# Moving the close of the state sums from VectorE to ScalarE and GpSimd, and six more convolutions to TensorE, in a fused attention, FFN, Mamba and LoRA block

## The chip, the core and the metric

The kernel runs on one core of a Trainium2 chip, in one launch. The metric is the device time of an execution in microseconds, the median over the runs. All arithmetic is fp32 (some matmuls split a value in two parts of fp32r).

## The reference

The input x is 4 x 256 x 512. A first layer adds a latent attention and an FFN of 1792 units; a second layer adds a Mamba block and a router with eight LoRA experts. The change touches only the Mamba block, which for each of the four sequences computes

```python
x, z = jnp.split(hidden_states @ in_proj_w, 2, axis=-1)      # 1024 channels each
for k in range(K):                                           # K = 4 taps in time
    xc = xc + conv_w[None, :, k:k + 1] * xp[:, :, k:k + Lq]
xc = silu(xc)                                                # xc began as conv_b
dt_r, Bm, Cm = rmsnorm of three parts of x_proj_w @ xc       # 32, 16, 16 rows
dt = softplus(dt_proj_w @ dt_r + dt_bias)
h = exp(dt * A) * h + dt * B_t * x_t                         # 16 states a channel, over 256 steps
y = sum over states of h * C_t
y = (y + D * xc) * silu(z)
out = y @ out_proj_w.T
```

## The kernel before

The order of all work is written out by hand: no scheduler moves an instruction, and each engine works its own queue in order. The first layer takes the first 330 us or so and is not touched. Its last matmuls (the FFN's second product, L469) run on into the first steps of what follows.

**Tiles of the Mamba block.** The 1024 channels of a sequence are eight chunks of 128 (DC = 8), and two chunks are a pair (p from 0 to 3). The 16 states are taken four at a time, so that a chunk is four steps (NU = 4) and a sequence 32 steps (PER). Step u belongs to sequence b = u // 32, chunk c = u % 32 // 4 and state group g = u % 4. There are 128 steps. In one step the 128 partitions hold 4 states x 32 channels, and the free axis 4 groups of channels x 256 points in time.

**One step** is, by engine:
- ScalarE: `decays`, four exponentials of 128 x 255 (L958), done two steps ahead, into one of three buffers;
- VectorE: `scan_in`, the product bx in PSUM (L964), then `scan`, the scan h over 128 x 1024 (L979); h has two buffers;
- GpSimd: hc = h * C (L984); hc has three buffers;
- TensorE: `states_sum`, one step later: four matmuls (L996), each of which sums the four states of 32 channels into its quarter of the one PSUM tile ysum. At a chunk's first step a matmul with the diagonal of D and xc (L994) opens ysum anew.

**The close.** When the four steps of a chunk are summed, `close_chunk` (L1000) multiplies ysum by silu(z) (tile sz, written by ScalarE in `gate_silu`, L932) on VectorE and writes the chunk of xcs over. It is issued between the product and the scan of the step two after the chunk's last one (u % 4 == 1). Until it is done TensorE can't open ysum for the next chunk. The output projection `out_mm` (L1088) reads the closed chunk.

**The next sequence's inputs.** While sequence b is scanned, the convolution of sequence b + 1 is made, in steps 5 to 20 of the 32:
- `px_mm` (L753): the input projection of a pair, into one PSUM tile px of 128 x 2 x 256;
- `conv_in`: ScalarE copies px to a padded tile (L762). For the pair's first chunk it scales the identity by the four taps, which gives four diagonals of 128 x 128 (L767). For the second chunk it writes the last tap with the bias (L768) and three scaled, shifted copies (L772);
- `conv_taps`, a step later: TensorE convolves the first chunk by four matmuls with the diagonals (L789), back into its half of px, and ScalarE adds the bias (L791). GpSimd adds the three copies of the second chunk (L795);
- `conv_silu` (L798), then the projection to dt, B and C: `pp_mm` (L809), `pp_square` (L815, L816), an inverse root on ScalarE (L708, L709) and on VectorE `pp_norm` (L823), which is issued after step 20's scan.

**Time steps.** `step_in` and `step_exp` (ScalarE) and `step_out` (GpSimd, L892 to L896, one instruction for each k) make dt for half a sequence; `step_x` (L903, GpSimd) makes du = dt * xc of a pair. Each sends its result to DRAM (L911), and `spread` (L917) loads it back in the layout of the steps, four DMAs for dt and four for du of a chunk, on SP's queue. On the same queue stand the loads of w_in (L621) and, in the first sequence, of the late weights rl, bw, lb and ow (L1206).

**The order** is two tables of step numbers, `at` (before the step's scan) and `late_at` (after it), filled by `put` and `put_late`; the main loop over u works them off.

Of the kernel before, what the change touches and what calls it, by code (L numbers as in the profile page):

```python
# [8 lines left out]
F32 = mybir.dt.float32  # L9

F32R = mybir.dt.float32r
AF = mybir.ActivationFunctionType
ALU = mybir.AluOpType
# [4 lines left out]
P = 128  # L18
B, S, D = 4, 256, 512
# [6 lines left out]
DIN, NST, KC, RK = 1024, 16, 4, 32  # L26
# [11 lines left out]
V_CW, V_CB, V_DB, V_AL, V_D, V_END = 0, 4, 5, 6, 22, 23  # L38
# [3 lines left out]
def block_kernel(  # L42
# [24 lines left out]
    nc = tc.nc  # L67
    mm = nc.tensor.matmul
# [15 lines left out]
    ident = cst[:, C_ID : C_ID + P]  # L84
# [34 lines left out]
    live = {}  # L119
# [22 lines left out]
    for i in range(2):  # L142
        t = ap1.tile([P, 2, 4, 32], F32, name=f"mpl{i}")
# [339 lines left out]
    def go(gen, n=1000):  # L483
        for _ in range(n):
            if next(gen, 1) == 1:
                break
# [138 lines left out]
    vec = we.tile([P, DC, V_END], F32, name="vec")  # L625
# [16 lines left out]
    w1 = ctx.enter_context(tc.tile_pool(name="w1", bufs=1, side="right"))  # L642
# [7 lines left out]
    NU = NST // NG  # L650
    PER = DC * NU
    xcs, nrms, dts, szs, crows = {}, {}, {}, {}, {}
# [27 lines left out]
    pads = []  # L680
    for i in range(2):
        t = w1.tile([P, 2, KC - 1 + S], F32, name=f"pad{i}")
# [12 lines left out]
    ysum = psy.tile([P, S], F32, name="ysum")  # L695
# [52 lines left out]
    def px_mm(b, p, i):  # L748
# [3 lines left out]
        for hc in range(HC):  # L752
            mm(px[:, i, :], lhsT=w[:, i, hc, :], rhs=xns[b][:, hc, :],  # L753
               start=(hc == 0), stop=(hc == HC - 1))

    def conv_in(b, p):


        px = live["px", b, p]
        if p == 0:  # L760
            xcs[b] = (act if b % 3 else w1).tile([P, DC, S], F32, tag=f"xc{b % 3}", name="xc")
        nc.scalar.copy(pads[p % 2][:, :, KC - 1 :], px)  # L762
        v = [vec[:, 2 * p + i, :] for i in range(2)]
        if b:
            dg = live["dg"] = w1.tile([P, KC, P], F32, tag="dg", name="dg")
            for k in range(KC):
                nc.scalar.activation(dg[:, k, :], ident, AF.Identity, scale=v[0][:, V_CW + k : V_CW + k + 1])  # L767
        nc.scalar.activation(xcs[b][:, 2 * p + 1, :], px[:, 1, :], AF.Identity,  # L768
                             bias=v[1][:, V_CB : V_CB + 1], scale=v[1][:, V_CW + KC - 1 : V_CW + KC])
        tp = w1.tile([P, KC - 1, S], F32, tag="tap", name="tap")  # L770
        for k in range(KC - 1):
            nc.scalar.activation(tp[:, k, :], pads[p % 2][:, 1, k : k + S], AF.Identity,  # L772
                                 scale=v[1][:, V_CW + k : V_CW + k + 1])
        live["tap"] = tp
        if b == 0:
            nc.scalar.activation(px[:, 0, :], px[:, 0, :], AF.Identity, bias=v[0][:, V_CB : V_CB + 1],
                                 scale=v[0][:, V_CW + KC - 1 : V_CW + KC])

    def conv_taps(b, p):
        px, c = live["px", b, p], 2 * p  # L780
        if b == 0:
            for k in range(KC - 1):
                nc.vector.scalar_tensor_tensor(
                    px[:, 0, :] if k < KC - 2 else xcs[b][:, c, :], pads[p % 2][:, 0, k : k + S],
                    vec[:, c, V_CW + k : V_CW + k + 1], px[:, 0, :], ALU.mult, ALU.add,
                )
        else:
            for k in range(KC):
                mm(px[:, 0, :], lhsT=live["dg"][:, k, :], rhs=pads[p % 2][:, 0, k : k + S],  # L789
                   start=(k == 0), stop=(k == KC - 1))  # L790
            nc.scalar.activation(xcs[b][:, c, :], px[:, 0, :], AF.Identity,  # L791
                                 bias=vec[:, c, V_CB : V_CB + 1])
        xc = xcs[b][:, c + 1, :]
        for k in range(KC - 1):
            nc.gpsimd.tensor_tensor(xc, xc, live["tap"][:, k, :], ALU.add)  # L795

    def conv_silu(b, z=None):
        nc.scalar.activation(xcs[b], xcs[b], AF.Silu)  # L798
# [143 lines left out]
    def lend(n, u):  # L942
        tag = lent[n][u]
        pool, bufs = (we, 3) if tag == "w_in" else (w1, 1)
        return pool.tile([P, NG, S], F32, tag=tag, name=n, bufs=bufs)

    def decays(u):
        b, c, g = u // PER, u % PER // NU, u % NU
        if u >= len(lent["d"]):
            da = decay[(u - 4) % 3]  # L950
        elif lent["d"][u] == "d":
            da = decay[0]
        else:
            da = lend("d", u)
            nc.gpsimd.memset(da[:, :, 0:1], 0.0)
        live["da", u] = da
        for k in range(NG):
            nc.scalar.activation(da[:, k, 1:], live["dts", b, c][:, k, 1:], AF.Exp,  # L958
                                 scale=aneg[:, c, k, g : g + 1])

    def scan_in(u):
        b, c, g = u // PER, u % PER // NU, u % NU
        bx = psx.tile([P, NG, S], F32, tag="bx", name="bx")
        nc.vector.tensor_tensor(  # L964
            bx, brow[g // 2][:, g % 2, :].unsqueeze(1).to_broadcast([P, NG, S]), live["dus", b, c], ALU.mult
        )
        live["bx"] = bx

    def scan(u, parts=1):
        b, c, g = u // PER, u % PER // NU, u % NU  # L970
        da, bx = live.pop(("da", u)), live["bx"]
        if u < len(lent["h"]):
            h, hc = lend("h", u), lend("hc", u)
        else:
            h = act.tile([P, NG, S], F32, tag="h", name="h", bufs=2)
            hc = act.tile([P, NG, S], F32, tag="hc", name="hc", bufs=3)
        for k in range(parts):
            n = slice(k * NG // parts, (k + 1) * NG // parts)
            nc.vector.tensor_tensor_scan(  # L979
                h[:, n].rearrange("p n t -> p (n t)"), da[:, n].rearrange("p n t -> p (n t)"),  # L980
                bx[:, n].rearrange("p n t -> p (n t)"), 0.0, ALU.mult, ALU.add,
            )

            (nc.vector if k == NG - 1 else nc.gpsimd).tensor_tensor(  # L984
                hc[:, n], h[:, n],
                crows[b][:, g, :].unsqueeze(1).to_broadcast([P, NG // parts, S]), ALU.mult,
            )
        live["hc", u] = hc
# [7 lines left out]
            mm(ysum[k * NB : (k + 1) * NB, :], lhsT=stack, rhs=hc[:, k, :],  # L996
               start=False, stop=(g == NU - 1))

    def close_chunk(b, c):
        nc.vector.tensor_tensor(  # L1000
            xcs[b][:, c, :], ysum, szs[b, c // 2][:, c % 2, :], ALU.mult
        )


# [82 lines left out]
    def out_mm(b, i, c):  # L1087
        mm(live["po", b, i], lhsT=xcs[b][:, c, i * P : (i + 1) * P], rhs=late_w["ow"][:, c, :],  # L1088
           start=False, stop=(c == DC - 1))
# [31 lines left out]
    px = live["px", 0, 3]  # L1121
    nc.scalar.copy(pads[1][:, :, KC - 1 :], px)
    for i in range(2):
        v = vec[:, 6 + i, :]
        nc.scalar.activation(px[:, i, :], px[:, i, :], AF.Identity, bias=v[:, V_CB : V_CB + 1],
                             scale=v[:, V_CW + KC - 1 : V_CW + KC])
# [33 lines left out]
    u, e, lw = live["u"], live["e"], live["lw"]  # L1160
# [15 lines left out]
    for i in range(2):  # L1176
        pdu = psmm.tile([P, 2, S], F32, tag="mm", name="pdus")
        for k in range(2):
            mm(pdu[:, k, :], lhsT=sel[:, (2 * i + k) * P : (2 * i + k + 1) * P], rhs=du[:, 0, :],
               start=True, stop=True)  # L1180
# [31 lines left out]
    def put(b, s, f, *a):  # L1212
        at.setdefault(b * PER + s, []).append((f, a))
# [5 lines left out]
    for b in range(B):  # L1219
# [36 lines left out]
        put(b, 2 if b else 6, step_in, b, 1, 1)  # L1256
        put(b, 3 if b else 7, step_exp, b, 1)

        for q, us in enumerate(((5, 6, 7), (10, 12, 14)) if b else ((8, 9, 11), (15, 17, 18))):
            for k in range(3):  # L1260
                put(b, us[k], step_out, b, 1, q, k)
        for p, u in ((2, 8 if b else 13), (3, 16 if b else 19)):
            put(b, u, step_x, b, p)
        for c in range(2, DC):
            o = 0 if b or c < 4 else 2
            put(b, 3 if c == 2 and not b else 4 * c - 6 + o, spread, "dt", b, c)
            put(b, 4 * c - 4 + o, spread, "du", b, c)
        put(b, 10, load_z, b, 2)
# [6 lines left out]
        if nxt < B:  # L1275
            o = 0 if b else 1
# [54 lines left out]
    total = B * PER  # L1331
    late = []
    for u in range(total + 2):
        if 3 <= u < total - 2:
            decays(u + 2)
        for f, a in at.get(u, ()):
            f(*a)
        if u < total:
            if u:
                scan_in(u)  # L1340
        last = u - 2
        if last >= 0 and last % NU == NU - 1:
            c = last % PER // NU
            close_chunk(last // PER, c)
            if last // PER == B - 1:
                late.append(c)
        if u < total:
            scan(u, 1 if u < total - 1 else 4)
            if u < 3:
                decays(u + 2)  # L1350
        for f, a in late_at.get(u, ()):
            f(*a)
        if late and u >= total - PER + 22:
            c = late.pop(0)
            for i in range(2):
                out_mm(B - 1, i, c)
        if 1 <= u <= total:
            states_sum(u - 1)
        if u < 3:
            go(ff, (9, 12, 100)[u])  # L1360
        if u == 2:
            open_act()
# [105 lines left out]
```

## Time and profile before

| | |
|---|---|
| runs | 850.30, 850.35 and 854.58 us; median 850.35 |
| profiled execution | 852.26 us, span 850.5 us, mean granted TensorE clock 0.954 |
| busy in the span | PE 740.6 (87%), VectorE (DVE) 669.6 (79%), ScalarE (ACT) 538.6 (63%), GpSimd (POOL) 489.1 (58%) |
| scan L979 | 125 of 128 x 1024, 2.284 us each |
| product L964 | 128, 1.232 us each |
| close L1000 | 32, 0.416 us each |
| hc L984 | 130, 2.322 us each |
| addition L795 | 45, 0.73 us each |

In a timeline a row has the start and the duration in us, the engine, the line, the operation, out<-in with their shapes, and how many instructions were merged; in brackets stands how long the engine was idle before it and what ended that. A row of waits has who waited for whom, the total in us, the times and the longest. A matmul of fp32 gives two records (x8 is four matmuls). The chain of waits is followed back from the last instruction.

### The profile page before, as it was taken

The numbers are of one execution on the slowest core, as the hardware profiler recorded it, in microseconds if no ns is written. First come the engines' busy times: TensorE is split into PE (matmuls) and PEld (weight loads), VectorE is DVE, ScalarE is ACT, GpSimd is POOL, SyncE is SP. The second block draws the span as 40 slices with busy tenths as digits, with TensorE's granted clock in tenths as the row PEclk, the third lists the DMA queues.
The fourth block names the chain that finished last, engine by engine and source line by source line (L and its number), as shares of the span: only waits on it lengthen the run. The fifth ranks groups of instructions, "written<-read, shape, count | busy, mean of one in ns | idle before, by whom it ended". The sixth has DMA issues, their size and how long they took to land.

```text
span 850.5 us, 10982 instructions
## 1 busy us (share of the span) xinstructions
PE 740.6 (87%) x3798; PEld 423.6 (50%) x3798; DVE 669.6 (79%) x647; ACT 538.6 (63%) x1061; POOL 489.1 (58%) x376
## 2 busy tenths in 40 slices
PE   5999999989999899989778888887898997956875
PEld 3565546656555676656444346344356444312331
DVE  4597755478744435798799999899999999999996
ACT  4225565223566267599885789786888885855561
POOL 3223322001343333669967689869599759697664
PEclk9999999899999999999898999989999979998998
DMA  7234332001222322555751644433553343443400
GB/s 223 68 94 125 88 86 62 0 1 38 75 75 79 113 56 63 139 147 161 206 142 50 173 137 124 123 100 109 156 155 99 102 112 102 109 119 105 112 25 25
DMA packets 67202, 86.71 MB, mean 102 GB/s; under 512 B 12061, under 2 KB 52009, under 8 KB 66762
## 3 DMA queue, kind: packets, MB, share of 16 engines
q1 hardware_dynamic: 57786, 67.12, 28.5%
q0 software_dynamic: 9072, 18.35, 7.8%
q8 instruction: 30, 0.49, 0.2%
q10 hardware_dynamic: 288, 0.52, 0.2%
q14 instruction: 26, 0.21, 0.1%
HBM read 66.58 MB, written 10.22 MB: 90 GB/s over the span
## 4 chain that ended last, share of the span: by engine, by line
PE 37%; DVE 30%; POOL 12%; ACT 8%; issue 6%; DMA 4%; SPq 1%; DVEq 0%; POOLq 0%; ACTq 0%
DVE h L979 18%; POOL hc L984 7%; PE pu L444 6%; PE pg L444 6%; DVE bx L964 6%; ACT decay L958 4%; PE av L397 4%; PE po L469 3%; PE scT L386 2%; DVE mpl L354 2%; PE px L753 2%; POOL xc L795 2%; PE pz L926 2%; DMA dus<-dud 2%; PE ysum L996 1%
## 5 line engine op out<-in xcount | busy, mean ns | idle before, releaser
L984 POOL TENSOR_TENSOR hc<-h,cr 128x1024 f32<-128x1024 f32 (+1 forms) x130 | 301.6, 2322 | 96.4 <-DVE h L979 76.6
L979 DVE TENSOR_TENSOR_SCAN h<-decay,bx 128x1024 f32<-128x1024 f32 (+1 forms) x129 | 288.0, 2234 | 16.3 <-PE po L469 4.0
L958 ACT ACTIVATE decay<-dts,aneg 128x255 f32<-128x255 f32 x504 | 213.3, 498 | 97.5 <-DVE h L979 87.2
L964 DVE TENSOR_TENSOR bx<-brow,dus 128x1024 f32<-128x1024 f32 x128 | 157.7, 1232 | 8.7 <-DMA dus<-dud 4.6
L996 PE MATMUL ysum<-hc,stack 128*32 128x256 f32 x1024 | 88.1, 413 | 60.1 <-POOL hc L984 59.8
L456 POOL TENSOR_TENSOR hlo<-g,hhi 128x512 fp32r<-128x512 f32 x28 | 35.9, 1281 | 118.3 <-ACT hhi L455 118.3
L427 POOL DMA_DIRECT2D wgu<-in_wgu x56 | 31.2, 558 | 97.3 <-PE pg L444 95.9
L354 DVE TENSOR_REDUCE mpl<-sc 128x4 f32<-128x1024 f32 x64 | 76.4, 1217 | 12.4 <-PE sc L352 12.2
L996 PEld LDWEIGHTS ysum<-hc,stack 128*32 128x32 f32 x1024 | 21.2, 111 | 120.7 <-POOL hc L984 98.1
L388 ACT ACTIVATE pe<-scT 128x1024 f32<-128x1024 f32 x64 | 64.0, 1023 | 23.4 <-PE sc L352 16.8
L1088 PE MATMUL po<-ow,xc 128*128 128x512 f32 x128 | 70.4, 659 | 2.2 <-DVE xc L1000 2.2
L926 PE MATMUL pz<-xn1T,w_in 128*128 128x256 f32 x256 | 67.5, 411 | 0.0
L753 PE MATMUL px<-xn1T,w_in 128*128 128x256 f32 x256 | 61.8, 387 | 0.1
L926 PEld LDWEIGHTS pz<-xn1T,w_in 128*128 128x128 f32 x256 | 49.0, 200 | 19.0 <-issue 10.8
L753 PEld LDWEIGHTS px<-xn1T,w_in 128*128 128x128 f32 x256 | 48.2, 192 | 13.1 <-issue 4.3
L452 DVE SCALAR_TENSOR_TENSOR g<-g,pg 128x512 f32<-128x512 f32 x28 | 19.2, 686 | 41.5 <-ACT g L451 41.5
L444 PE MATMUL pu<-xhi,wgu 128*128 128x512 f32 x112 | 48.7, 435 | 2.3 <-DMA wgu<-in_wgu 2.3
L469 PE MATMUL po<-wd,hhi 128*128 128x512 f32 x112 | 50.3, 449 | 0.0
L444 PE MATMUL pg<-xhi,wgu 128*128 128x512 f32 x112 | 48.9, 437 | 0.0
L455 ACT CAST hhi<-g 128x512 fp32r<-128x512 f32 x28 | 17.3, 619 | 48.5 <-DVE g L454 48.5
L444 PE MATMUL pu<-xlo,wgu 128*128 128x512 f32 x112 | 45.4, 405 | 0.0
L469 PE MATMUL po<-wd,hlo 128*128 128x512 f32 x112 | 45.0, 401 | 0.0
(230 smaller groups left out, 1251.7 us busy)
## 6 DMA issues: line engine op xcount, KB each, us to landing
dts<-dtd SPq DMA_DIRECT2D x124, 128.0 KB, 2.9
dus<-dud SPq DMA_DIRECT2D x124, 128.0 KB, 3.0
wgu<-in_wgu POOLq DMA_DIRECT2D x56, 256.0 KB, 2.8
w_in<-in_inx SPq DMA_DIRECT2D x16, 512.0 KB, 4.3
w_in<-in_inz SPq DMA_DIRECT2D x16, 512.0 KB, 4.9
dtd<-dt SPq DMA_DIRECT2D x15, 256.0 KB, 2.2
dud<-du SPq DMA_DIRECT2D x15, 256.0 KB, 2.2
wd<-in_wd POOLq DMA_DIRECT2D x7, 512.0 KB, 3.6
```

What stands on the lines that cost most here:

```text
L354: nc.vector.tensor_reduce(mpl2[b % 2][:, qb, 2 * hp : 2 * hp + 2, 16 + 2 * gq : 18 + 2 * gq], sc.rearrange("p i (f k) -> p i f k", f=2), A ...
L388: nc.scalar.activation(pes[b, k][:, 2 * t : 2 * t + 2, :], sc, AF.Exp)
L444: mm(ps, lhsT=wgus[i][:, hc, :], rhs=xs[j][:, hc, :], start=(hc == 0 and j == 0), stop=(hc == HC - 1 and j == 1))
L469: mm(po, lhsT=hids[th][j][:, m, i * P : (i + 1) * P], rhs=wd[:, m, :], start=False, stop=(m == MC - 1 and j == 1))
L753: mm(px[:, i, :], lhsT=w[:, i, hc, :], rhs=xns[b][:, hc, :], start=(hc == 0), stop=(hc == HC - 1))
L926: mm(pz[:, i, :], lhsT=w[:, i, hc, :], rhs=xns[b][:, hc, :], start=(hc == 0), stop=(hc == HC - 1))
L958: nc.scalar.activation(da[:, k, 1:], live["dts", b, c][:, k, 1:], AF.Exp, scale=aneg[:, c, k, g : g + 1])
L964: nc.vector.tensor_tensor(bx, brow[g // 2][:, g % 2, :].unsqueeze(1).to_broadcast([P, NG, S]), live["dus", b, c], ALU.mult)
L979: nc.vector.tensor_tensor_scan(h[:, n].rearrange("p n t -> p (n t)"), da[:, n].rearrange("p n t -> p (n t)"), bx[:, n].rearrange("p n t -> ...
L984: (nc.vector if k == NG - 1 else nc.gpsimd).tensor_tensor(hc[:, n], h[:, n], crows[b][:, g, :].unsqueeze(1).to_broadcast([P, NG // parts, ...
L996: mm(ysum[k * NB : (k + 1) * NB, :], lhsT=stack, rhs=hc[:, k, :], start=False, stop=(g == NU - 1))
L1088: mm(live["po", b, i], lhsT=xcs[b][:, c, i * P : (i + 1) * P], rhs=late_w["ow"][:, c, :], start=False, stop=(c == DC - 1))
```

## The change

- `take_sum` copies ysum into the chunk of xcs: on ScalarE, at the very start of the step, ahead of that step's exponentials; for the first chunk of the first sequence on VectorE, after the product.
- `gate` multiplies that by sz on GpSimd, after the step's hc.
- The last chunk of the last sequence is still closed by one multiplication on VectorE. In the last sequence a closed chunk is queued for `out_mm` one step later.
- For six pairs (b, p), two in each of the sequences 1 to 3, the second chunk too gets four diagonals (in the tile of the taps), four matmuls into its half of px, and a copy with bias by ScalarE. The additions by GpSimd remain for the other pairs.
- In the first sequence step_out, step_x and the spreads of chunks 4 to 7 get other steps.

```diff
+    both = ((1, 0), (1, 3), (2, 1), (2, 3), (3, 1), (3, 3))
 def conv_in(b, p):
...
+        tp = live["tap"] = w1.tile([P, KC - 1, S], F32, tag="tap", name="tap")
+        if (b, p) in both:
+            tp = tp.rearrange("p k t -> p (k t)")
+            for k in range(KC):
+                nc.scalar.activation(tp[:, k * P : (k + 1) * P], ident, AF.Identity,
+                                     scale=v[1][:, V_CW + k : V_CW + k + 1])
+        else:
+            (L768 and the three L772, as before)
 def conv_taps(b, p):
...
+        if (b, p) in both:
+            dg = live["tap"].rearrange("p k t -> p (k t)")
+            for k in range(KC):
+                mm(px[:, 1, :], lhsT=dg[:, k * P : (k + 1) * P], rhs=pads[p % 2][:, 1, k : k + S],
+                   start=(k == 0), stop=(k == KC - 1))
+            nc.scalar.activation(xc, px[:, 1, :], AF.Identity, bias=vec[:, c + 1, V_CB : V_CB + 1])
+        else:
+            (the three L795, as before)
-    def close_chunk(b, c):
-        nc.vector.tensor_tensor(
-            xcs[b][:, c, :], ysum, szs[b, c // 2][:, c % 2, :], ALU.mult
+    def take_sum(b, c):
+        (nc.scalar.copy if b or c else nc.vector.tensor_copy)(xcs[b][:, c, :], ysum)
+    def gate(b, c):
+        nc.gpsimd.tensor_tensor(
+            xcs[b][:, c, :], xcs[b][:, c, :], szs[b, c // 2][:, c % 2, :], ALU.mult
         )
-        for q, us in enumerate(((5, 6, 7), (10, 12, 14)) if b else ((8, 9, 11), (15, 17, 18))):
+        for q, us in enumerate(((5, 6, 7), (10, 12, 14)) if b else ((9, 10, 11), (13, 15, 16))):
             for k in range(3):
                 put(b, us[k], step_out, b, 1, q, k)
-        for p, u in ((2, 8 if b else 13), (3, 16 if b else 19)):
+        for p, u in ((2, 8 if b else 11), (3, 16 if b else 17)):
             put(b, u, step_x, b, p)
         for c in range(2, DC):
-            o = 0 if b or c < 4 else 2
+            o = 0 if b or c < 4 else 1
             (spread dt at step 4c - 6 + o, spread du at 4c - 4 + o)
 for u in range(total + 2):
+        last = u - 2
+        shut = (last // PER, last % PER // NU) if last >= 0 and last % NU == NU - 1 else None
+        if shut and shut != (0, 0) and u < total:
+            take_sum(*shut)
         (decays of step u + 2, the step's table, product)
-        last = u - 2
-        if last >= 0 and last % NU == NU - 1:
-            c = last % PER // NU
-            close_chunk(last // PER, c)
-            if last // PER == B - 1:
-                late.append(c)
+        if shut == (0, 0):
+            take_sum(0, 0)
+        if u > total:
+            b, c = shut
+            nc.vector.tensor_tensor(xcs[b][:, c, :], ysum, szs[b, c // 2][:, c % 2, :], ALU.mult)
         (scan and hc)
+        if shut and u < total:
+            gate(*shut)
         (the late table, output matmuls of the last sequence)
+        if shut and shut[0] == B - 1:
+            late.append(shut[1])
```

## The prediction

> **What bounds the kernel now.** I read the chain of waits first, then VectorE's timeline one step at a time, VectorE's waits, the busy times by stretch, and last the timelines of ScalarE and TensorE where the first sequence convolves the second one's inputs. From 333 us on the work is 128 steps of one product (L964) and one scan (L979).
>
> ```profile
> DVE h L979 18%; POOL hc L984 7%; PE pu L444 6%; PE pg L444 6%; DVE bx L964 6%; ACT decay L958 4%; PE av L397 4%; PE po L469 3%; PE scT L386 2%; DVE mpl L354 2%; PE px L753 2%; POOL xc L795 2%; PE pz L926 2%; DMA dus<-dud 2%; PE ysum L996 1%
> ```
>
> L979 and L964 hold 24% of the span, GpSimd's hc 7%. One ordinary step and one with a close, in VectorE's timeline:
>
> ```profile
> 489.95 1.23 DVE L964 TENSOR_TENSOR bx<-brow,dus 128x1024 f32<-128x1024 f32 x1
> 491.32 2.29 DVE L979 TENSOR_TENSOR_SCAN h<-decay,bx 128x1024 f32<-128x1024 f32 x1
> 493.64 1.23 DVE L964 TENSOR_TENSOR bx<-brow,dus 128x1024 f32<-128x1024 f32 x1
> 494.78 0.41 DVE L1000 TENSOR_TENSOR xc<-ysum,sz 128x256 f32<-128x256 f32 x1
> 495.11 2.27 DVE L979 TENSOR_TENSOR_SCAN h<-decay,bx 128x1024 f32<-128x1024 f32 x1
> 497.42 1.23 DVE L964 TENSOR_TENSOR bx<-brow,dus 128x1024 f32<-128x1024 f32 x1
> ```
>
> The ordinary step takes 493.64 - 489.95 = 3.69 us, the one with the close 3.78: the close of 0.41 us costs 0.09. Without it the scan starts 491.32 - 491.18 = 0.14 after its product ends, and the close fills that gap and overlaps both neighbours. 127 steps of 3.69 are 468.6; the products of steps 0 and 127 start at 333.05 and 838.92, 505.9 apart. So 37.2 us are lost. About 16 of them are the closes themselves and these waits:
>
> ```profile
> DVE xc L1000 <- PE ysum L996: 8.5, 6, 2.9
> DVE bx L964 <- DMA dus<-dud: 4.6, 2, 3.2
> DVE xc L1000 <- ACT sz L932: 1.2, 1, 1.2
> ```
>
> The rest is VectorE's own work (two routings of 4.6 us, normalization sums) and one wait of 4.0 for L469. The waits of closes lie in the first sequence (1.18 at step 5, 1.17 at 9, 2.87 at 13), the second (1.82 at 49, 0.53 at 57), the third (1.39 at 81) and the tail (0.71); both DMA waits are in the first, at steps 16 and 20.
>
> ```profile
> core 0: us, PE busy (x) PEld busy (x) DVE busy (x) ACT busy (x) POOL busy (x), PEclk, DMA share, GB/s
> 355.00:412.00 57.00, 50.33 (x288) 35.19 (x287) 46.53 (x30) 53.98 (x121) 45.69 (x33) 0.94 0.60 177
> 480.00:540.00 60.00, 51.50 (x279) 30.34 (x278) 57.37 (x38) 52.20 (x122) 53.54 (x35) 1.00 0.43 123
> 725.00:842.00 117.00, 86.00 (x413) 33.46 (x411) 112.74 (x74) 67.85 (x143) 84.78 (x41) 0.93 0.30 81
> ```
>
> This decides the case. In 355 to 412 ScalarE, not VectorE, is the full engine (53.98 of 57.00); later VectorE is (57.37 of 60, 112.74 of 117).
>
> **The change part by part.** *Closes leave VectorE.* Thirty multiplications go, the first chunk's becomes a copy there, which no longer waits for sz (0.8 us sooner at step 5). Some 24 of the 30 did not wait: 24 x 0.09 = 2.2 us, not 30 x 0.415 = 12.5. The Trainium skill ("VectorE: DVE Perf Modes", The DRAIN you can't avoid) lets the next operation start only when the pipe is empty and advises few operations; by that each close would be worth its full 0.41 and this part 12.5 us. The rows say 0.09, and I keep them.
>
> *ScalarE copies the sums:* 30 copies, nearest row L791 (0.47, 128x256 from PSUM), lowest row L1072's plain copy (0.35). Each stands ahead of the next step's four exponentials (1.7 us). In the fourth sequence those end 7.1 before their scan: hidden; with no such cover the thirty would cost 14.1.
>
> *GpSimd gates:* 31 x 0.729 (L795's row) = 22.6 us, less 18 additions of the six pairs, 13.1. It sits behind hc, and its reader is an output matmul a step or more later: hidden as long as VectorE sets the pace, and 9.5 if GpSimd did. A step of GpSimd's is 2.36 + 1.27 = 3.63 with step_out's part, 4.70 with three additions, against 3.69: that is how hc falls from 2.5 to 5.6 us behind the scan over steps 40 to 47, and why step 49 waits. From 37 to 48 GpSimd's work is 12 x 2.36 + 8 x 1.27 + 12 x 0.729 = 47.2 against 44.3 of VectorE's; with six additions and three gates in place of twelve additions it is 45.1. The lag then stays under the 5.07 (two steps less one scan) at which h's two buffers hold the scan, and what is late next is ScalarE.
>
> *Both chunks by TensorE, six pairs.* ScalarE: out go L768 and three taps (0.55 + 1.50), in come four diagonals (4 x 0.394) and a copy (0.47): nothing. TensorE gets four matmuls, 2.00 us (L789's four at full clock). But there is a new wait. L789 writes one half of px and waits for L768, which reads only the other:
>
> ```profile
> 380.03 1.28 ACT L767 ACTIVATE dg<-cst,vec 128x128 f32<-128x128 f32 x4
> 381.21 0.55 ACT L768 ACTIVATE xc<-px,vec 128x256 f32<-128x256 f32 x1
> 381.81 2.84 PE L789 MATMUL px<-pad,dg 128*128 128x256 f32 x8 [2.05 <-ACT xc L768]
> ```
>
> By the same rule the second four matmuls wait for the copy of the first half; that copy is queued behind a step's exponentials; and ScalarE then stands until they are done: 2.05 us of ScalarE per pair, behind which are the next exponentials, and on TensorE px and the sums. The Trainium skill ("PSUM — Partial Sum Buffer", Terms) says why: two engines must not touch one bank at once, and px's two halves fill one. No run here shows what happens without that wait. Bounds of the 2.05: nothing if ScalarE had to wait anyway, as for L791 at 536.30 (2.55 idle); 4.0 if TensorE has fallen to half clock, as after the 2.05 idle above, where four matmuls took 2.84 and the next 2.77 instead of 1.99. I take 2.05, the full-clock row.
>
> *First sequence sooner.* step_out, du and the spreads move one to two steps earlier, with their DMAs. On SP's queue dud is no longer behind the loads of w_in and lb: at 397.99 it was issued, 1.4 after du was done. dus for step 16 still stands behind the w_in load that TensorE's px frees (397.04), so it is issued near 400 instead of 403.41. This takes the 3.18 and 1.43 off VectorE.
>
> **The sum by sequence.** First: up to 5.2 + 4.6 come off VectorE, but ScalarE's queue up to the inverse root, which VectorE needs at L823, gets longer: three sums 1.41, two copies 0.94, diagonals for taps -0.95, two waits 4.1, the third sum behind the router's matmuls about 1.0, less the 1.68 idle before 411.47 that vanishes: +4.8.
>
> ```profile
> 423.71 0.42 ACT L709 ACTIVATE rs<-rs 64x256 f32<-64x256 f32 x1
> 427.60 0.45 DVE L823 SCALAR_TENSOR_TENSOR nrm<-pp,lnw,rs 64x256 f32<-64x256 f32 x1
> ```
>
> The margin is 427.60 - 424.13 = 3.5. So L823 comes 1.3 later, and everything gained before is given back there. L809's sixteen passes took 5.58 at half clock where 3.9 is the usual: if they don't, L823 is 0.3 sooner. At half clock in both pairs it is 5.3 later. I take 1.0 later, then two closes, 0.2 back.
> Second: six closes 0.5, step 57's 0.75; of step 49's 2.04 (538.22 to 541.62 against 1.36) ScalarE, some 2.4 later through the second matmuls and copy plus 0.4 for the sum, delivers step 51's exponentials about 1 too late (they ended 545.08, scan 548.98): 1.0 kept. 2.3.
> Third: 0.5 + 0.3, and 0.7 of step 81's 1.6: 1.5. Fourth: 8 x 0.09 = 0.7. The tail is unchanged: its last close stays on VectorE.
> Sum: -1.0 + 0.2 + 2.3 + 1.5 + 0.7 = 3.7. The profiled execution took 852.26 (span 850.5), 1.9 over the median of the runs, 850.35; 852.26 - 3.7 is 848.6 for its like, and 846.6 against the median. 0.5%, 4.25 us, is about what can be told from no change.
>
> **Rivals.** *ScalarE keeps up in the first sequence* (0.20): for it, each wait on TensorE may fall where ScalarE stood anyway; against it, 53.98 of 57.00. Then nearly all of 8.5 - 0.7 + 1.2 + 4.6 + 2.2 = 15.8 comes, of which ScalarE after the silu withholds 2: 834 to 842, by the sum 836.5.
> *The shared bank of px decides* (0.14), the slower side: each pair halts ScalarE for 4.0, not 2.05, since TensorE, idle some 2.5 us before, runs its second four at half clock. Two such halts fall on the first sequence's chain, one each on the second's and third's: 4 x (4.0 - 2.05) = 7.8 against the 3.7: 854.5 to 858. It turns slower from 2.05 + 3.7/4 = 3.0 us per halt.
> *The wait only moves* (0.08): a close's wait for ysum becomes a gate's wait on GpSimd or a wait before the exponentials, nothing is gained but 2.2 at most: 848 to 850.4. Against: those exponentials have 5 to 7 us to spare outside the silu.
>
> **How the numbers follow.** Forecast 0.58, 842 to 850, 846.6 likeliest; 846.1 divides it, 0.26 faster and 0.32 same. The first rival gives 0.19 and 0.01, the second 0.14 slower, the third 0.08 same. Faster 0.45, same 0.41, slower 0.14. The range 837 to 855.5 leaves out about half of each outer rival.
>
> **What would show it.** Steps with chunk ends at 3.69, not 3.78; no wait of L964 for dus; no L1000-like waits on VectorE but step 5's and the tail's. ScalarE idle about 2 us before each second copy, six times, ended by TensorE. VectorE waiting for decays near step 16 and for rs before L823; hc no more than 3.5 behind the scan in steps 40 to 47. I am wrong if L823 comes early and without a wait (first rival), or if those halts are over 3 us (second).

## The result and the profile after

The changed kernel takes 862.56 us (median of 858.32, 862.54, 862.58 and 862.60), the kernel before 850.33 beside it: ratio 1.011 with a 95% interval of 1.007 to 1.015. (The quotient of these two medians is 1.014; single runs lie over 4 us apart, and I go by the interval.) It is slower by about 9 us, against a forecast of 3.7 faster. Single runs of one kernel differ by up to 11 us, in part because the untouched first layer hands over to step 0 at 330.2 to 334.8 us in the profiled executions (granted clock 0.94 to 0.97 over its first 200 us). So beside each ratio I give the **scan time** of the profiled execution: from the start of step 0's product to that of step 127's. Before it is 838.92 - 333.05 = 505.87, after 849.02 - 333.44 = 515.58, which is 9.7 more. A scan time comes from one execution, so a microsecond or two of it is not shown to repeat. One slow run (1039.31 us, of the kernel with the closes on VectorE) is in no ratio.

The lines that answer to those shown of before. The chain of waits:

```profile
DVE h L994 9%; ACT decay L973 7%; PE pg L444 6%; PE po L469 6%; PE pu L444 5%; PE px L753 5%; PE av L397 4%; PE ysum L1011 4%; POOL hc L999 4%; PE po L1107 3%; PE pz L941 3%; PE scT L386 2%; DVE bx L979 2%; PE pp L824 2%; DVE mpl L354 2%
```

The scan fell from 18% to 9% of it and ScalarE's exponentials rose from 4% to 7%: the end is now set by who feeds VectorE. The busy times by stretch:

```profile
core 0: us, PE busy (x) PEld busy (x) DVE busy (x) ACT busy (x) POOL busy (x), PEclk, DMA share, GB/s
355.00:412.00 57.00, 52.46 (x282) 36.01 (x280) 43.20 (x27) 52.38 (x119) 44.22 (x30) 0.91 0.61 176
725.00:842.00 117.00, 88.64 (x434) 37.04 (x430) 111.65 (x64) 75.45 (x163) 93.20 (x52) 0.95 0.36 96
```

In the first stretch VectorE is busy for 43.20 instead of 46.53: two closes of 0.42 have left it, and for the rest it waits more. In the second, the fourth sequence, it is still full, and the sums and gates lie beside it on ScalarE (75.45, 67.85 before) and GpSimd (93.20, 84.78 before). Step 41, which had a close, in VectorE's timeline:

```profile
513.11 1.23 DVE L979 TENSOR_TENSOR bx<-brow,dus 128x1024 f32<-128x1024 f32 x1
514.48 2.29 DVE L994 TENSOR_TENSOR_SCAN h<-decay,bx 128x1024 f32<-128x1024 f32 x1
516.80 1.23 DVE L979 TENSOR_TENSOR bx<-brow,dus 128x1024 f32<-128x1024 f32 x1
```

516.80 - 513.11 = 3.69, not 3.78: the 0.09 per close is there. Five of the rows of VectorE's waits show what came in its place:

```profile
DVE h L994 <- ACT decay L973: 7.6, 4, 2.5
DVE bx L979 <- DMA dus<-dud: 6.3, 1, 6.3
DVE h L994 <- POOL hc L999: 5.2, 3, 3.6
DVE m L1054 <- ACT ml L1032: 5.1, 2, 3.1
DVE xc L1369 <- PE ysum L1011: 1.0, 1, 1.0
```

Of the closes only the tail's still waits for sums, and the first chunk's copy (0.42 at step 5), as the change means it. But the scan waits for exponentials and for hc, the routing (m, of the logits ml) waits for ScalarE's copy, and the one wait for dus is longer than the two of before (4.6). VectorE also waits twice for the inverse root rs, 1.50 at step 20 and 1.05 at step 52. ScalarE's own waits:

```profile
ACT xc L1016 <- PE ysum L1011: 20.3, 11, 3.8
ACT xc L807 <- PE px L805: 12.5, 6, 2.1
```

The second is the **halt**: six of 2.08, as costed. Its place, on ScalarE and on TensorE:

```profile
386.27 0.47 ACT L799 ACTIVATE xc<-px,vec 128x256 f32<-128x256 f32 x1
388.83 0.48 ACT L807 ACTIVATE xc<-px,vec 128x256 f32<-128x256 f32 x1 [2.09 <-PE px L805]
```

```profile
386.79 2.00 PE L805 MATMUL px<-pad,tap 128*128 128x256 f32 x8 [2.02 <-ACT xc L799]
```

TensorE is idle for 2.02 until ScalarE gets to the first copy, which stands behind four exponentials; then ScalarE is idle for 2.09. Each engine waits in turn for the other over one tile. In the other five pairs TensorE waited 0.6 to 0.9 there.

Where the 9.7 us lie (differences of the scan time's parts, sequence by sequence):

| | first | second | third | fourth | sum |
|---|---|---|---|---|---|
| predicted | +0.8 | -2.3 | -1.5 | -0.7 | -3.7 |
| after | +4.4 | +0.8 | +5.2 | -0.7 | +9.7 |

### The profile page after: what moved, and what is told of

Its sections match the earlier page's. It is cut to its first block, busy times and chain, and to the rows that moved or that the text cites. A ratio compares the mean times of both kernels' runs of the same rounds, so it can differ in the third digit from the quotient of the medians.

```text
span 860.8 us, 11089 instructions
## 1 busy us (share of the span) xinstructions
PE 759.3 (88%) x3846; PEld 435.6 (51%) x3846; DVE 662.9 (77%) x617; ACT 546.9 (64%) x1097; POOL 496.4 (58%) x389
## 4 chain that ended last, share of the span: by engine, by line
PE 55%; DVE 17%; ACT 15%; POOL 6%; issue 3%; DMA 3%; SPq 1%; ACTq 0%; DVEq 0%; POOLq 0%
DVE h L994 9%; ACT decay L973 7%; PE pg L444 6%; PE po L469 6%; PE pu L444 5%; PE px L753 5%; PE av L397 4%; PE ysum L1011 4%; POOL hc L999 4%; PE po L1107 3%; PE pz L941 3%; PE scT L386 2%; DVE bx L979 2%; PE pp L824 2%; DVE mpl L354 2%
## 5 line engine op out<-in xcount | busy, mean ns | idle before, releaser
L941 PE MATMUL pz<-xn1T,w_in 128*128 128x256 f32 x256 | 72.6, 434 | 0.0
L941 PEld LDWEIGHTS pz<-xn1T,w_in 128*128 128x128 f32 x256 | 52.6, 216 | 22.1 <-issue 12.8
```

What stands on the lines that cost most here:

```text
L941: mm(pz[:, i, :], lhsT=w[:, i, hc, :], rhs=xns[b][:, hc, :], start=(hc == 0), stop=(hc == HC - 1))
```

## The experiments

Lines of the kernels with eight matmuls first are 3 higher (L808 and L810 are their two copies). All scan times are against 505.87.

| kernel | ratio to before, 95% | scan time |
|---|---|---|
| closes, pairs and steps (the change) | 1.0109 (1.0066 to 1.0152) | +9.7 |
| closes and steps, no pairs | 1.0007 (0.9979 to 1.0035) | +1.9 |
| pairs and steps, closes on VectorE | 1.0088 (1.0054 to 1.0123) | +5.1 |
| closes and pairs, old steps | 1.0076 (1.0043 to 1.0108) | +8.5 |
| closes only | 1.0040 (1.0009 to 1.0070) | +0.7 |
| steps only | 0.9996 (0.9967 to 1.0026) | -0.4 |
| the change, eight matmuls first | 0.9982 (0.9954 to 1.0010) | +0.6 |
| the change, sums behind the exponentials | 1.0151 (1.0101 to 1.0200) | +12.7 |
| pairs only, eight matmuls first | 1.0022 (0.9995 to 1.0049) | +0.9 |
| the change, eight first, logits sooner | 0.9967 (0.9939 to 0.9996) | -2.1 |
| the same with sums behind the exponentials | 1.0068 (1.0039 to 1.0098) | +10.7 |
| the same with all closes on VectorE | 1.0016 (0.9985 to 1.0046) | +2.4 |
| the same with some closes on VectorE | 0.9979 (0.9949 to 1.0009) | -3.4 |

**One part undone at a time.**

```diff
-    both = ((1, 0), (1, 3), (2, 1), (2, 3), (3, 1), (3, 3))
+    both = ()
```

> The changed kernel without its six pairs (both = (), so the second chunk of every pair goes through ScalarE's taps and GpSimd's additions again); the sums' copies, the gates and the new steps stay. Three theories. (A) The halts: in the changed kernel ScalarE stands 2.08 us before each second copy and needs 0.48 for it, and the silu, the inverse root and the logits' copies behind it come late. Then this run loses the waits of VectorE for rs and ml at steps 20 to 22 (about 5 of the 5.9 us lost there), the 1.8 and 1.2 of the second sequence and the 2.5 and 2.8 of the third, some 12 us; 18 additions more on GpSimd beside the gates give up to 3 back: 850 to 854 us. (B) The sums: the copy of the sums stands in front of the exponentials and ScalarE waits there for TensorE (1.4 us at step 9, 2.8 at step 65). Then most of the loss stays: 857 to 860. (C) The new steps of the first sequence are at fault: only the second and third sequence get better, 857 to 859, and the step 16 to 22 loss of 5.9 stays.

Measured 854.24 us, just over (A)'s range, where before had 854.69 on that chip. The loss is gone, as (A) says; (B) and (C) miss. But the gates stand ahead of hc together with all the additions, and this kernel's waits of VectorE show the price in all three sequences that convolve, more of it than the 3 that (A) foresaw, though the scan time is up by 1.9 only:

```profile
DVE h L994 <- POOL hc L999: 13.3, 13, 2.8
```

> The changed kernel with the closes on VectorE as in the kernel before (one multiplication between product and scan); six pairs and new steps stay. (A) The halts: ScalarE still stands 2.08 six times; without the sums' copies it is some 1.5 to 2.5 us sooner in the first sequence, the closes cost 2.2 on VectorE and their waits come back: 860 to 863. (B) The sums: the 1.4 us stand and three copies go in the first sequence, the 2.3 at step 70 and its 2.8 stand go in the third: 854 to 857. (C) The new steps: 861 to 864.

The edit puts L1000 of before back and takes `take_sum` and `gate` out. Measured 861.77 us: inside (A), but inside (C) too, so this run parts only these two from (B); the run after it speaks against (C). In its first sequence VectorE loses nothing (scan time -0.0 by step 32, against +4.4), although ScalarE halts twice there. Halts without the moved closes cost the first sequence nothing, moved closes without halts 0.8 (the run before this one), both together 4.4. That fits one margin on ScalarE that they share, the 3.5 us before the normalization L823 (L838 here). The third sequence loses 3.6 here.

> The changed kernel with the first sequence's old step numbers for step_out, du and the spreads; closes and pairs as changed. (A) and (B): nothing at the silu of the first sequence changes, which sets the end there; what the waits for dus at steps 16 and 20 take is again hidden behind the late inverse root: 861.5 to 865. (C) The new steps (additions in GpSimd's queue ahead of hc at step 12, and SP's queue) are at fault: 856 to 858.

The three lines of step numbers are those of before. Measured 861.53 us, as (A) and (B) say: the new steps are not what made it slow. This profile has no wait at step 70, where the changed kernel's has one of 2.3. There four output matmuls took 3.78 us where they take 1.98 here, and the sums behind them came late. So about 2 of the 5.2 in the third sequence may belong to that one execution: TensorE's granted clock was 0.61 and 0.54 from 604 to 612 us there. One trace of each can't show whether the change brought it.

**The halt itself.**

```diff
-            (4 matmuls of the first half, copy L799, 4 matmuls of the second, copy L807)
+            (4 matmuls of the first half, 4 of the second, both copies)
```

> The changed kernel with the order inside the six pairs turned: all eight diagonal matmuls first, then both copies by ScalarE. TensorE no longer waits for the first copy, and ScalarE has one wait at most in place of two. (A) The halts: in the first pair of each sequence (1,0), (2,1), (3,1) and in (1,3) the first copy hardly waited (0, 0.2, 0.5, 0), so there 2.1 us each go; in (2,3) and (3,3) the first copy waited 1.9 already, and the two together wait 4.0 as before. The first sequence gets back 4 of its 5 us: 857 to 859, and the waits at steps 51 and 83 stay. (B) and (C): 861 to 863.

Measured 852.73 us where before had 854.69, better than (A) expected: same instructions, another order, and 9.1 us of scan time less (some 7 if the wait at step 70 is left out). The place shown above is now, on ScalarE:

```profile
386.21 0.47 ACT L808 ACTIVATE xc<-px,vec 128x256 f32<-128x256 f32 x1 [0.17 <-PE px L806]
386.59 0.47 ACT L810 ACTIVATE xc<-px,vec 128x256 f32<-128x256 f32 x1
```

0.17 us of waiting in place of 2.09. That is the best of the six: ScalarE's waits for px in the six pairs were 0.2, 1.4, 2.2, 3.4, 2.0 and 3.4, together 12.5. In the changed kernel they were 17.0, with the 4.5 before the first copies; and TensorE's 5.1 us of idle before the second four are gone. By sequence the scan time stands at -1.4, +1.5, +1.2 and -0.7: the order's cost was in the first and third. The wait at step 83, expected to stay, fell from 2.5 to 0.7. The one at step 51 stayed (1.8), as expected, since in pair (2,3) ScalarE has to wait for eight matmuls either way.

**The sums' place.**

```diff
-        take_sum(*shut)   # ahead of decays(u + 2)
         decays(u + 2)
+        take_sum(*shut)
```

> The changed kernel with the copy of the sums behind the step's four exponentials instead of ahead of them; halts, pairs and new steps stay. (A) The halts alone make the loss: the order of the two changes nothing that is late, the copies still stand in ScalarE's queue: within 1.5 us of the changed kernel, a ratio to the kernel before of 1.009 to 1.011. (A+B) Halts and sums together overfill ScalarE: the waits of ScalarE for TensorE's sums (1.4 at step 9, 2.8 at step 65) are hidden behind the 1.7 of exponentials, the first sequence's inverse root comes 1.4 sooner and the wait of 2.3 at step 70 goes: 3.5 to 5 us less than the changed kernel, a ratio of 1.004 to 1.007.

Measured 863.81 us, ratio 1.0151: neither. The first half came true: its first sequence lost 2.6 instead of 4.4, and step 70 had no wait (nor had it with the old steps). But this kernel's waits of GpSimd show what I had left out:

```profile
POOL xc L1019 <- ACT xc L1016: 11.5, 4, 5.4
```

The gate waits for the copy, and the next hc stands behind the gate. That the sums stand ahead of the exponentials is not the fault of the change: behind them they cost 3 us more.

**Pairs and closes by themselves.** The next kernel is the one before with the six pairs and eight matmuls first.

> The kernel before with only the six pairs, and in them all eight matmuls first, then both copies; closes on VectorE and old steps as before. (A) The halts were all that was bad in the pairs: GpSimd is rid of 18 additions, the close's wait of 1.8 at step 49 and some of the 1.4 at step 81 go, and ScalarE's longer way to the silu (two copies less taps, up to 2 us) stays inside its margin of 3.5: 1.5 to 3.5 us faster than before, ratio 0.996 to 0.998. (D) The pairs are bad even so, since ScalarE still stands up to 4 us in pairs (2,3) and (3,3) for eight matmuls: 1 to 4 slower than before, ratio 1.001 to 1.005.

1.0022: (D) rather than (A), though not to be told from 1. Its first two sequences gain 1.5 and 1.4 us of scan time; the third loses 3.8, all at step 85: the close waits 1.7 for sums, then the routing 1.1 for logits, and the subtraction after it takes 1.21 instead of 0.19 (see the last section). I put the two waits down to the 3.6 us that ScalarE stands in pair (3,3) at step 80; no run shows that link.

> The kernel before with only the closes moved (sums copied by ScalarE, gated by GpSimd); no pairs, old steps. (A) The halts alone made the loss, so the moved closes by themselves gain what the rows of the kernel before promise (the waits at steps 9, 13, 49, 57, 81 and 24 x 0.09): 2 to 5 us faster, ratio 0.994 to 0.998. (G) GpSimd is full in the steps with additions, and each gate of 0.73 stands ahead of the next hc, so VectorE waits for h's buffer as often as it waited for the sums: no gain, ratio 0.999 to 1.004.

1.0040, (G)'s upper end. The waits for sums go but for 1.1 us, and 12 waits for hc (9.1 us) come.

> The kernel before with only the first sequence's new steps. By the prediction's own term the waits for dus at steps 16 and 20 (3.2 and 1.4) go, and of these 4.6 us 3.5 are kept at the normalization, whose inverse root was ready that much earlier: ratio 0.996. If the last logits, which ScalarE copied only 0.6 us before VectorE read them, come in front of that, 0.6 is kept: ratio 0.999 to 1.000. If dus does not land sooner, since the same loads stand ahead of it in the DMA queue: 1.000.

0.9996, as the second case has it. The waits for dus fell from 4.6 to 2.1, not to none, and by step 20 the kernel was 2.6 ahead; at step 22 it was 0.3 ahead. The normalization kept the gain, the routing a step later lost it. VectorE's timeline, then GpSimd's:

```profile
428.75 0.19 DVE L1035 TENSOR_REDUCE m<-ml 128x4 f32<-128x32 f32 x1 [0.30 <-ACT ml L1013]
428.97 2.03 DVE L1036 TENSOR_TENSOR ex<-ml,m 128x32 f32<-128x32 f32 x1
430.92 1.22 DVE L964 TENSOR_TENSOR bx<-brow,dus 128x1024 f32<-128x1024 f32 x1
```

```profile
428.59 2.35 POOL L984 TENSOR_TENSOR hc<-h,cr 128x1024 f32<-128x1024 f32 x1 [1.67 <-DVE h L979]
```

0.3 is the late logits; L1036 took 2.03 instead of 0.19 and ended when hc did (more below).

**Toward a better kernel.** The changed kernel's routing waited 2.09 before step 22 and 3.06 before step 86. The first, in VectorE's timeline, behind the normalization that was late already:

```profile
430.39 0.48 DVE L838 SCALAR_TENSOR_TENSOR nrm<-pp,lnw,rs 64x256 f32<-64x256 f32 x1 [1.50 <-ACT rs L709]
430.80 1.22 DVE L979 TENSOR_TENSOR bx<-brow,dus 128x1024 f32<-128x1024 f32 x1
432.11 2.29 DVE L994 TENSOR_TENSOR_SCAN h<-decay,bx 128x1024 f32<-128x1024 f32 x1
436.49 0.18 DVE L1054 TENSOR_REDUCE m<-ml 128x4 f32<-128x32 f32 x1 [2.09 <-ACT ml L1032]
```

With eight matmuls first, the router's matmuls move ahead:

```diff
-                for i, u in enumerate((16, 19, 20, 21)):
+                for i, u in enumerate((16, 19, 19, 20)):
```

> The eight-first order again, and beside it the router's third and fourth matmuls a step sooner (steps 16, 19, 19, 20 in place of 16, 19, 20, 21), so that ScalarE copies the last logits ahead of the projections that wait for the normalized rows. If the last logits' place behind eight other operations of ScalarE is what VectorE waits for at step 22 (2.1 us) and step 86 (3.1), these 5.1 go, less what waits next (rs, up to 1.5 each): 2 to 5 us less than the eight-first order alone, a ratio to the kernel before of 0.992 to 0.996. If that wait only stands for the late inverse root, nothing is gained: 0.998.

848.71 us where before had 853.76: ratio 0.9967, 0.9939 to 0.9996, so this version beats both kernels, the one before only just. The gain is smaller than expected (0.992 to 0.996): 2.7 us of scan time less than eight first alone, which the two ratios can't tell apart; the wait before step 22 is gone, of that before step 86 0.5 is left.

> All three together: eight matmuls first, the sums' copy behind the exponentials, the router's matmuls a step sooner. (A) As the run with eight first and sooner logits, within 1 us. (A+B) The remaining waits for exponentials at steps 51 (1.8) and 83 (0.7) shrink by the 0.4 of a copy each and the first sequence's queue to the inverse root by up to 1.4: 1 to 2.5 less than that run.

1.0068: worse by 12.7 us of scan time than with the sums ahead; both expectations fall, for the reason found above (its gates wait 11.2 us for the copy, four times).

> Eight matmuls first, new steps and the logits a step sooner, with all closes on VectorE as before. If a close costs VectorE 0.09 us and the moved sums and gates cost ScalarE and GpSimd more than that, this beats the same kernel with sums and gates (ratio 0.997): the 0.5 to 1.2 us waits for hc at steps 58 to 61 and the wait for exponentials at step 51 go (4 us), and waits of closes for ysum of some 4 come: ratio 0.992 to 0.996. If moving the closes was worth 4 us or more by itself: 0.998 to 1.002.

1.0016, scan time +2.4 against -2.1 with sums and gates moved: the last case named. The closes wait 12.1 us for sums. So with ScalarE relieved of the halts and the logits sooner, moving the closes is worth 4.5 us of scan time; the intervals of the two ratios overlap a little.

```diff
+        dve = bool(shut) and (shut[0] == 0 or u > total or shut in ((1, 5), (1, 6)))
```

> The same with the closes of the first sequence and of chunks 5 and 6 of the second on VectorE, the others copied by ScalarE and gated by GpSimd. If each place is cheapest where the rows show its engine free (ScalarE is full in the first sequence, GpSimd at steps 56 to 62): 1.5 to 3.5 us less than the version with all sums and gates moved, ratio 0.992 to 0.995; if the places do not matter, 0.996 to 0.997.

0.9979 (0.9949 to 1.0009), scan time -3.4; the ratio fits neither case. The waits for hc at steps 58 to 61 went, but by the runs it can't be told from the version before it.

## Why the prediction was wrong

The terms that held: 0.09 a close (-0.7 in the fourth sequence for eight; by the rule of the Trainium skill's "VectorE: DVE Perf Modes", The DRAIN you can't avoid, it would have been 8 x 0.41 = 3.3); six halts of 2.05 (2.08); hc's lag at steps 40 to 47 under the limit of 5.07 (up to 4.3, where I said 3.5); the wait at step 49 gone, worth 2.0; the tail unchanged; dus issued near 400 (401.69).

The halts came as forecast, in number and length. The step that failed is the overlap: how much of them VectorE would not feel. My sum charged the 2.05 only twice in full, on ScalarE's way to L823, where the margin of 3.5 left 1.3 of the whole queue's 4.8 (I took 1.0), and about 1 us at step 51; and it had the kernel turn slower only from 3.0 us per halt. At 2.08 it was slower already: the kernel with eight matmuls first says that this order cost 7 to 9 us. The second rival was right that the halts decide, but not about why: TensorE ran the second four matmuls at full clock. Neither sign of being wrong appeared (no halt over 3 us; L838 late and behind a wait of 1.50), so those signs did not cover this way of failing. What I did not follow was ScalarE's lateness past the first engine it meets:

- *First sequence, +0.8 said, +4.4 measured.* The silu's table load came 418.65 - 413.19 = 5.5 late and rs 6.2, against 4.8 in the sum: one sum's copy stood 1.4 waiting for TensorE at step 9, and L824's passes took 6.36 after an idle of 3.56 (5.58 before). L838 was 2.8 later (2.4 counted from step 0's product), where the sum has 1.0. Then came the last logits, which I never costed. They had 0.6 us to spare before the change (copied at 431.06, read at 431.63), and VectorE waited 2.09 for them.
- *The waits for dus, 4.6 said to vanish.* They became one of 6.3. On SP's queue, before and after, and the product of step 16 that waits:

```profile
397.04 0.38 SPq L621 DMA_DIRECT2D w_in<-in_inz  x1
403.41 1.75 SPq L917 DMA_DIRECT2D dus<-dud  x4
407.78 1.23 DVE L964 TENSOR_TENSOR bx<-brow,dus 128x1024 f32<-128x1024 f32 x1 [3.18 <-DMA dus<-dud]
```

```profile
400.74 0.38 SPq L621 DMA_DIRECT2D w_in<-in_inz  x1
401.69 1.80 SPq L932 DMA_DIRECT2D dus<-dud  x4
410.49 1.23 DVE L979 TENSOR_TENSOR bx<-brow,dus 128x1024 f32<-128x1024 f32 x1 [6.35 <-DMA dus<-dud]
```

Issued 1.7 sooner, dus let the product start 2.7 later. I had the issue right and the landing wrong, in two ways. Issued 0.95 behind the load of w_in instead of 6.4, dus took 6.8 to 7.4 from issue to landing, 2.5 to 3.0 before. And that load was itself issued 3.7 later: SP's queue had stood longer at the load of w_in ahead of it, which waits for TensorE's px (issued at 390.55, 387.25 before), and then at dts, which waits for dtd to land. (So it is not px that freed the load at 397.04, as the prediction reads it, but the end of dts.) Counted from step 0's product, dus in the kernel with new steps only was issued 5.3 sooner and the product started 1.4 sooner; in the changed kernel without pairs the product started 1.3 sooner, with them 2.3 later.
- *GpSimd.* Late taps held its additions for 3.9 at 389.6, hc stood behind them, and step 14's scan waited 3.64 for a buffer of h. The wait for dus at step 16 covered that one; but the prediction had followed hc's lag at steps 40 to 47 only, and the later such waits count.
- *Second sequence, -2.3 said.* Step 51's exponentials cost 1.8, not 1.0; rs made VectorE wait 1.1, and hc 1.6 at steps 60 and 61, where the gates meet step_out.
- *Third, -1.5 said.* 2.5 at step 83 for exponentials and 3.1 for logits before step 86, the kinds of wait met before, and the 2.3 of step 70.

The forecast's idea that closes leave VectorE at a gain showed only with eight matmuls first and the logits sooner (4.5 us). With all additions on GpSimd there was none (closes only, 1.0040), and with the halts the scan time was 4.6 more with the closes moved than with them on VectorE (+9.7 against +5.1; the ratios 1.0109 and 1.0088 can't be told apart).

## What to carry to other kernels

Where the matmuls into one half of a tile must wait for the copy of the other half, try all matmuls first and all copies after: here alternating them made ScalarE idle for 2.1 us and TensorE for 0.6 to 2.0 per tile, and turning the order gained 7 to 9 us without one instruction less. Price a delay on a busy in-order engine by every reader of its queue, the smallest margin first (0.6 us for logits here), not by the one reader that looks critical. A DMA issued sooner gains little if a large load is issued just ahead of it (with the new steps only, dus was issued 5.3 us sooner and used 1.4 sooner). A small operation moved to another engine must be weighed with what stands behind it there: the gate took 0.73 us itself, and the hc behind it set the scan.

## What the runs showed of the hardware

VectorE's subtraction L1036 (128x32, both inputs and the output in SBUF) takes 0.19 us, but where GpSimd's hc was running when it came, it lasted until hc's end: 428.97 + 2.03 = 431.00 against 430.94 in the kernel with new steps only. In the kernel with eight first and logits sooner it took 1.84 at 676.89, to 678.73, and hc ended at 678.69. The reduction just before it, with one input, took its usual 0.16 to 0.19 meanwhile. The Trainium skill ("SBUF — State Buffer", SBUF: two separate sides) says that an operation of VectorE with two SBUF inputs and one of GpSimd shut each other out for a whole instruction; the numbers agree. No run took the hc away from that place, so this rests on the coincidence of the ends.

An idle of about 2 us did not always bring half clock: L805's four matmuls took 2.00 after 2.02 of idle (granted clock 1.00 from 384 to 392 us), where before L789's took 2.84 after 2.05 (0.85 and 0.72 from 380 to 388). The Trainium skill ("TensorE: Matmul & The Clock Gate", What's actually happening) has the clock fall after an idle window of about 3.4 us, and the windows run freely. The second case fell with less idle than that, so this rule does not explain it, and no run here does.
